# Layer 2 of a four-layer model: dense experts against experts over gathered tokens

## The chip, the cores and the metric

The kernel runs on one core of a Trainium2 chip. The metric is the device time of one execution in microseconds, the median of several runs. Five engines work side by side, each on its own stream of instructions in order: PE multiplies matrices into PSUM, DVE and ACT do elementwise work and read PSUM, POOL does elementwise work in SBUF and issues indirect transfers, SP issues the other transfers. Semaphores tie them together.

## What is computed

The input x has 16 batches of 256 tokens and 256 features; everything is float32. Four layers follow each other, each an attention part and a feed-forward part added to x: layer 0 with top-2 routing over eight experts of limited capacity, layer 1 with eight gated experts and a shared one, layer 3 with a projection in simulated 8-bit floats. The feed-forward part of layer 2 is itself a causal self-attention followed by four unlike experts, of which each token uses two:

```python
logits = jnp.nan_to_num(xf @ gate_w.T)
probs = jax.nn.softmax(logits, axis=-1)
topv, topi = jax.lax.top_k(probs, K)                    # K = 2 of E = 4
topv = topv / (topv.sum(-1, keepdims=True) + 1e-08)
wts = jnp.zeros((N, E), x.dtype).at[jnp.arange(N)[:, None], topi].add(topv)
o0 = _gelu(xf @ e0_up.T) @ e0_down.T
o1 = jax.nn.silu(xf @ e1_w1.T) * (xf @ e1_w2.T) @ e1_down.T
o2 = _gelu(_gelu(_gelu(xf @ e2_l1.T) @ e2_l2.T) @ e2_l3.T) @ e2_l4.T
o3 = _gelu(_gelu(xf @ e3_down.T) @ e3_up.T) @ e3_out.T
moe = wts[:, 0:1] * o0 + wts[:, 1:2] * o1 + wts[:, 2:3] * o2 + wts[:, 3:4] * o3
moe = moe.reshape(B, T, C).at[:, :, :M].set(0.0)        # M = 64
return x + moe
```

## The kernel before

Each layer is a software pipeline over batches. A hand-written list, `order`, has entries (position, function, lag, arguments). The loop runs over steps s and calls each function in order of position for batch s minus lag, where that batch exists. In the layers with such a list PE, DVE, ACT and POOL execute exactly in this order of calls; transfers on SP keep their program order too. A lag of 2 means that the function works on a batch two steps after that batch's lag-0 functions.

In layer 2 (L1097 on) a step holds, for the newest batch, the cross attention (`X[b]`, a `Heads32` object: `exps`, `added`, `values`, then `x_back`, which transposes its result back and adds it to x), then at lag 0 `statistics`, `norm`, `turned`, `project`, `head_squares`, `head_scale`, `heads_k`, `heads_q` and four `maxima` of the causal self-attention. At lag 1 follow four `exps`, `values`, `back`, `out_project` (which leaves the normalised tokens in `hh`) and `experts_in` (their transpose `xf`). The gate's logits, `route` and `routed` (the weights `wts`) come at lags 1 to 2.

`exps` masks the causal triangle after the exponential, by an affine select on POOL; `maxima` masks before, by a bf16 matmul of a triangle with the identity. `added` sums the exponentials of the two halves of the keys on POOL, so that `values` needs the product with ones once; without it, `values` multiplies both halves.

The experts are `work`, a list of units. Every unit fills one PSUM bank with two `f_part` calls and empties it with `f_end`: gelu on ACT, or silu as a tanh on ACT and two products on DVE, or for the last layer of an expert `f_add`, which multiplies by `wts` and adds into x. All four experts run on all 256 tokens of a batch, at lag 2, spread evenly over the step's positions. Their weights are streamed in 14 parts per batch by `fetch` and `part` through seven buffers `fw`. Four PSUM banks serve attention, two the experts. `f_done` stores x to DRAM (`xd2`) at lag 3.

Layer 3 loads x with `prepare`, four steps ahead of its attention. Layer 1's results reach layer 2 as in-flight row gathers, `x_fetch`, from `yslots`, an indirect transfer on POOL. Layer 0's `load` also clears DRAM buffers for later scatters, from a tile `zero`.

Of the kernel before, what the change touches and what calls it, by code (L numbers as in the profile page):

```python
# [36 lines left out]
def tile_kernel(ctx: ExitStack, tc: tile.TileContext, a, out):  # L37
# [72 lines left out]
    yslots = keep.tile([NBLK * BLK, D], F32, name="yslots")  # L110
    idx1 = ct([P, 2, NT], "idx1", U32)
# [287 lines left out]
    with ExitStack() as l01:  # L399
# [30 lines left out]
        with ExitStack() as l0:  # L430
# [47 lines left out]
            def load(b):  # L478
# [10 lines left out]
                if 2 <= b < 6:  # L489
                    for k in range(2):  # L490
                        dma(xe[k][(b - 2) * 1024 : (b - 1) * 1024, :].rearrange("(p r) d -> p (r d)", p=P), zero)
                        if b == 2:
                            dma(ye[k][8 * CAP :, :], zero[0:1, :D])
                if 6 <= b < 6 + (NBLK * BLK + 1023) // 1024:
                    rows = xslots[(b - 6) * 1024 : min((b - 5) * 1024, NBLK * BLK), :]
                    dma(rows.rearrange("(p r) d -> p (r d)", p=P), zero[:, : rows.shape[0] * 2])
# [120 lines left out]
            def scatter(b, n):  # L617
# [17 lines left out]
                (0, exps, 0, 0), (1, q_stats, -2), (2, back, 1, 0), (3, maxima, -1, 1), (4, scatter, 3, 1),  # L635
                (5, back, 1, 1), (6, values, 0, 0), (7, t_stats, 1), (8, exps, 0, 1), (9, queries, -1, 0, QMs),
                (10, maxima, -1, 2), (11, slots, 2), (12, values, 0, 1), (13, t_norm, 1), (14, exps, 0, 2),
                (15, q_norm, -2), (16, scatter, 5, 4), (17, maxima, -1, 3), (18, turned, 1), (19, values, 0, 2),
                (20, queries, -2, 0, QTs), (21, exps, 0, 3), (22, router, 1), (23, maxima, -2, 0), (24, route, 1),
                (25, load, -3), (26, queries, -1, 1, QMs), (27, values, 0, 3), (28, queries, -2, 1, QTs),  # L640
                (29, scatter, 3, 2), (30, v_heads, -2),
# [476 lines left out]
    with ExitStack() as l2:  # L1118
# [6 lines left out]
        wts = t2([P, NT, 4], "wts")  # L1125


        with ExitStack() as l2a:
            ca = l2a.enter_context(tc.tile_pool(name="ca", bufs=1))
            wp = at[0] = l2a.enter_context(tc.tile_pool(name="at2", bufs=2))  # L1130
            ring[0] = rings(at[0], 16)
# [11 lines left out]
            n2w = col(a["n2_w"], 2, "n2w", ca)  # L1143
# [17 lines left out]
            trif = ta([P, P], "trif")  # L1161
            V.memset(trif, 0.0)
            G.affine_select(trif, trif, [[-1, P]], ALU.is_ge, -MASKED, base=0, channel_multiplier=1)
            tri2 = ta([P, 2, P], "tri2", BF16)
            for i in range(2):
                V.tensor_copy(tri2[:, i, :], trif)
# [28 lines left out]
            def x_load(b):  # L1195
                ys[b] = []
                xs[b] = wp.tile([P, 2, D], F32, name="x2", tag="x2", bufs=6)
# [109 lines left out]
            def mask(sc, j, t):  # L1307
                T.matmul(
                    sc[:, :, t * P : (t + 1) * P], lhsT=ident_bf, rhs=tri2,
                    start=True, stop=False, skip_group_check=True,  # L1310
                )

# [9 lines left out]
            def exps(b, u):  # L1322
                pT = pTs[b, u] = probs(u // 2, u % 2, QMs[b], KTs[b], 32, 0.0, 1.0, None, None, True)
                q0 = u % 2 * P

                for e in pT:
                    G.affine_select(  # L1327
                        e[:, :, q0 : q0 + P], e[:, :, q0 : q0 + P], [[0, 2], [1, P]], ALU.is_ge, 0.0, base=0, channel_multiplier=-1
                    )
# [21 lines left out]
            def out_project(b):  # L1351
                xn, ss = xcs.pop(b), small(2, "ss")
                hh = hhs[b, 1] = wp.tile([P, 2, D], F32, name="hh", tag="hh")
# [23 lines left out]
            def experts_in(b):  # L1377
                xfs[b] = wp.tile([P, 2, S], F32, name="xf", tag="xf")
                transposed(xfs[b], hhs.pop((b, 1)), n2w, A)

            def gates(b):
                p, xf = ptr(), xfs[b]
# [19 lines left out]

            def routed(b):

                pr, w, m = routes.pop(b), wts[:, 2 * b : 2 * b + 2, :], small(2, "rm")
# [3 lines left out]
                oh = [sm.tile([P, 2, 4], F32, name=f"oh2{k}", tag=f"oh2{k}", bufs=2) for k in range(2)]  # L1409
                m12 = [small(2, f"m12{k}", bufs=2) for k in range(2)]  # L1410
                top2(pr, 2, 4, oh, m12)
                V.scalar_tensor_tensor(m, m12[0], 1e-8, m12[1], ALU.add, ALU.add)
                V.reciprocal(m, m)
                for k in range(2):
                    V.tensor_tensor(m12[k], m12[k], m, ALU.mult)
                    V.tensor_tensor(oh[k], oh[k], m12[k].unsqueeze(2).to_broadcast([P, 2, 4]), ALU.mult)
                V.tensor_tensor(w, oh[0], oh[1], ALU.add)
                V.tensor_scalar(w[:, :, 1], w[:, :, 1], 0.5, None, ALU.mult)
# [4 lines left out]
                ("e0_upT", 2, 0, 512), ("e2_l1T", 2, 0, 512), ("e0_downT", 4, M, D), ("e1_w1T", 2, 0, 512),  # L1423
                ("e2_l2T", 4, 0, 256), ("e2_l2T", 4, 256, 512), ("e1_w2T", 2, 0, 512), ("e1_downT", 4, M, D),
                ("e2_l3T", 4, 0, 256), ("e2_l3T", 4, 256, 512), ("e3_downT", 2, 0, D),
                ("e2_l4T", 4, M, D), ("e3_upT", 2, 0, 512), ("e3_outT", 4, M, D),
# [3 lines left out]
            def fetch():  # L1430
                n, k, n0, n1 = parts[len(fw) % len(parts)]
                t = fp.tile([P, 1024], F32, name="fw", tag="fw", bufs=7)
# [4 lines left out]
            def part(b, i):  # L1437
                n = len(parts) * b + i
                while len(fw) < min(n + 6, len(parts) * B):
# [3 lines left out]
            hs = {}  # L1443
# [4 lines left out]
            def f_up(b, p, j, src, i, f):  # L1448

                w = part(b, i)  # L1450
                src = xfs[b] if src is None else hs[src]
                src = [src[:, c, :] for c in range(2)] if not isinstance(src, list) else [h[:, c, :] for h in src for c in range(2)]
# [346 lines left out]
```

## Time and profile before

| | |
|---|---|
| median of 3 runs | 3467.52 us (3456.1 to 3470.55) |
| the profiled execution | 3460.77 us |
| its span, first to last instruction | 3459.1 us |
| PE busy | 3117.0 us, 90% |
| PE weight loads busy | 2283.7 us, 66% |
| DVE, ACT, POOL busy | 1578.2, 1162.5, 1064.4 us |
| moved by DMA | 332.87 MB, 96 GB/s on average |

By busy time and the layers' first instructions, layer 0's attention runs to about 430 us, its experts to 900, layer 1 to 1556, layer 2 to 2969, layer 3 to the end. Busy time is summed per engine over the span or over a window. A group's row gives line, engine, operation, output and input tiles, shape and count, then busy time, mean nanoseconds of one, and the idle time before it with what ended it. Matmul instructions overlap, so a group's busy time is less than its count times its mean; a float32 product is two instructions in these rows. Times are from one execution.

### The profile page before, as it was taken

What the parts mean: (1) busy time and instruction counts of PE and PEld (TensorE: products, weight loads), DVE (VectorE), ACT (ScalarE), POOL (GpSimd) and SP (SyncE); (2) the same over time, 40 slices, a digit from 0 to 9 for tenths busy, and PEclk for the clock granted to TensorE, in tenths of its full rate; (3) what the DMA queues carried; (4) which work ended last, traced back from release to release, by engine and by line L of the source; (5) the groups of instructions that cost most, each with busy time, mean ns of one, the idle gap of its engine ahead of it and who ended that gap; (6) DMA issues with size and microseconds to landing.
All of it is one profiled execution on the core that took longest, in us unless ns stands there. A gap on an engine that the chain in (4) does not pass through costs nothing. (4 is left out here: it accounts for less than half of the span.)

```text
span 3459.1 us, 54867 instructions
## 1 busy us (share of the span) xinstructions
PE 3117.0 (90%) x21640; PEld 2283.7 (66%) x21640; DVE 1578.2 (46%) x3920; ACT 1162.5 (34%) x2085; POOL 1064.4 (31%) x1643
## 2 busy tenths in 40 slices
PE   7999599999677999995799999999999999699983
PEld 4666366666465578882477777777777778566751
DVE  6777511000475322223445455555455442277766
ACT  3555321111122111111245555554555544122221
POOL 2455600000473510002233333333333221155552
PEclk9999799999988999996799999999999999899995
DMA  6411222121232366653023333333333234310101
GB/s 229 152 51 43 71 73 72 64 74 40 76 115 78 123 217 200 192 172 107 13 78 105 100 106 108 110 100 105 97 103 98 88 91 127 128 31 27 30 7 49
DMA packets 262132, 332.87 MB, mean 96 GB/s; under 512 B 20891, under 2 KB 214091, under 8 KB 259700
## 3 DMA queue, kind: packets, MB, share of 16 engines
q1 hardware_dynamic: 249588, 296.59, 27.2%
q0 software_dynamic: 12288, 32.78, 2.8%
q8 instruction: 171, 2.80, 0.3%
q14 instruction: 85, 0.70, 0.1%
HBM read 259.29 MB, written 70.80 MB: 95 GB/s over the span
## 5 line engine op out<-in xcount | busy, mean ns | idle before, releaser
L1454 PE MATMUL pf<-hf,fw 128*128 128x256 f32 x1280 | 302.5, 380 | 0.0
L1454 PE MATMUL pf<-xf,fw 128*128 128x256 f32 x1152 | 290.8, 390 | 0.0
L252 ACT ACTIVATE big<-pmm 128x512 f32<-128x512 f32 (+1 forms) x512 | 237.1, 549 | 116.3 <-PE pmm L245 115.7
L1454 PEld LDWEIGHTS pf<-hf,fw 128*128 128x128 f32 x1280 | 234.6, 190 | 31.8 <-issue 4.8
L1454 PEld LDWEIGHTS pf<-xf,fw 128*128 128x128 f32 x1152 | 207.7, 190 | 55.0 <-issue 27.7
L780 PE MATMUL pmm<-xiT,w 128*128 128x512 f32 x512 | 225.4, 598 | 5.4 <-DVE xiT L134 5.3
L1327 POOL TENSOR_SCALAR_AFFINE_SELECT big<-big 128x256 f32<-128x256 f32 x256 | 104.8, 426 | 393.4 <-ACT big L252 386.6
L788 PE MATMUL pacc<-w,h 128*128 128x256 f32 x1024 | 223.6, 379 | 0.0
L788 PEld LDWEIGHTS pacc<-w,h 128*128 128x128 f32 x1024 | 194.6, 190 | 33.3 <-issue 7.7
L816 POOL DMA_INDIRECT y<-ye,idx x64 | 65.5, 1024 | 479.3 <-issue 479.3
L789 DVE COPY yo<-pacc 128x256 f32<-128x256 f32 x64 | 27.2, 425 | 402.2 <-PE pacc L788 402.2
L305 DVE TENSOR_REDUCE max<-pmm 128x2 f32<-128x512 f32 x256 | 158.9, 683 | 91.6 <-PE pmm L223 91.1
L1481 PE MATMUL pf<-fw,hf 128*128 128x192 f32 x1024 | 191.2, 331 | 0.2
L1318 DVE TENSOR_REDUCE qpad<-pmm 128x2 f32<-128x256 f32 (+1 forms) x256 | 124.9, 551 | 137.6 <-PE pmm L223 137.6
L522 DVE TENSOR_REDUCE qpad<-pmm 128x2 f32<-128x512 f32 x256 | 158.9, 684 | 54.6 <-PE pmm L223 54.4
L338 POOL TENSOR_TENSOR big<-big 128x512 f32<-128x512 f32 x128 | 158.6, 1273 | 73.3 <-ACT big L252 73.3
L780 PEld LDWEIGHTS pmm<-xiT,w 128*128 128x128 f32 x512 | 96.2, 191 | 124.4 <-issue 112.3
L1481 PEld LDWEIGHTS pf<-fw,hf 128*128 128x128 f32 x1024 | 165.6, 190 | 13.7 <-issue 11.9
L1212 POOL DMA_INDIRECT y<-yslots,idx x64 | 66.7, 1043 | 315.2 <-DMA yslots<-yb 301.7
L355 DVE RECIPROCAL rT<-pacc 128x256 f32<-128x256 f32 x64 | 112.1, 1751 | 94.8 <-PE pacc L347 94.8
L1466 ACT ACTIVATE hf<-pf 128x512 f32<-128x512 f32 x176 | 104.8, 595 | 124.2 <-PE pf L1454 123.6
L146 POOL TENSOR_SCALAR rsq<-mv 128x2 f32<-128x2 f32 x128 | 25.1, 196 | 337.2 <-DVE mv L164 318.8
(383 smaller groups left out, 6164.7 us busy)
## 6 DMA issues: line engine op xcount, KB each, us to landing
w<-in_w_dram SPq DMA_DIRECT2D x16, 1024.0 KB
fw<-in_e_upT_dram SPq DMA_DIRECT2D x32, 512.0 KB
fw<-in_e_l2T_dram SPq DMA_DIRECT2D x32, 512.0 KB
fw<-in_e_l3T_dram SPq DMA_DIRECT2D x32, 512.0 KB
wg<-in_w_gate_dram SPq DMA_DIRECT2D x39, 352.0 KB
wu<-in_w_up_dram SPq DMA_DIRECT2D x39, 352.0 KB
fw<-in_e_downT_dram SPq DMA_DIRECT2D x32, 384.0 KB
wd<-in_w_down_dram SPq DMA_DIRECT2D x39, 256.0 KB
```

The costliest lines, as they stand in the source:

```text
L252: A.activation(e[:, :, q0:], sc[j], AF.Exp, bias=bias, scale=scale)
L305: V.tensor_reduce(self.m[:, t, j, :], sc, AX.X, ALU.max, negate=True)
L338: G.tensor_tensor(r, self.pT[0][j], self.pT[1][j], ALU.add)
L355: V.reciprocal(rT, p[:, 1, :])
L522: V.tensor_reduce(qps[b][t][:, 8 * cp + j : 8 * cp + j + 5 : 4, 17], sc, AX.X, ALU.max, negate=True)
L780: T.matmul(p, lhsT=w1[:, c, f * P : (f + 1) * P], rhs=xiT[:, c, :], start=(c == 0), stop=(c == 1))
L788: T.matmul(p[:, :D], lhsT=hT[f][:, s * P : (s + 1) * P], rhs=w2[:, f, :], start=(f == 0), stop=(f == 7))
L1318: V.tensor_reduce(qp[:, 8 * cp + j : 8 * cp + j + 5 : 4, 16], sc, AX.X, ALU.max, negate=True)
L1327: G.affine_select(e[:, :, q0 : q0 + P], e[:, :, q0 : q0 + P], [[0, 2], [1, P]], ALU.is_ge, 0.0, base=0, channel_multiplier=-1)
L1454: T.matmul(p[:, j * S : (j + 1) * S], lhsT=w[:, c, f * P : (f + 1) * P], rhs=x, start=(c == 0), stop=(c == len(src) - 1),)
L1466: A.activation(f_hidden(to, f), p, AF.Gelu)
L1481: T.matmul(p[:, t * S : t * S + D - M], lhsT=hs[src][f // 2][:, f % 2, t * P : (t + 1) * P], rhs=w[:, f, :], start=(f == 0), stop=(f == 3),)
```

## The change

The experts of layer 2 get only the tokens that chose them. DRAM buffers `xe2` and `ye2` hold 4096 rows for each expert; each pair of batches has 256 of them. `places` counts, by two matmuls with `before` and `ones`, each token's slot in the regions of its two experts. `scatter` writes the tokens to these slots by four indirect transfers a batch; `f_in` reads the 256 rows of a pair and an expert, `f_turned` transposes them, and the units run over them. `f_out` stores the results to `ye2`. A region that runs over continues in the next pair's 256 rows. Rows beyond 2048 are left to a new stage after the loop, which loads all expert weights and works in pieces of 128 to 512 rows, each behind a test of the expert's count.

Expert 2 runs at even steps and the other three at odd ones, at lags 4 and 5, some ends one step on. The loop has three more steps. In layer 3, `fetch` gathers each token's two result rows and `chosen` adds them, weighted. Further, `exps` masks by matmul, `added` is not called in layer 2, and the lists of layers 0 and 3 have new positions and lags.

```diff
+    xe2 = keep.tile([4 * REG, D], F32, name="xe2")
+    ye2 = keep.tile([4 * REG, D - 64], F32, name="ye2")
...
+                dma(xe2[b * 1024 : (b + 1) * 1024, :].rearrange("(p r) d -> p (r d)", p=P), zero)
+                n0 = b // 4 * REG + REG // 2 + b % 4 * 512
+                dma(ye2[n0 : n0 + 512, :].rearrange("(p r) d -> p (r d)", p=P), zero[:, : 4 * (D - 64)])
...
-                (0, exps, 0, 0), (1, q_stats, -2), (2, back, 1, 0), (3, maxima, -1, 1), (4, scatter, 3, 1),
...
+                (0, scatter, 3, 1), (1, back, 1, 0), (2, maxima, -1, 1), (3, back, 1, 1), (4, exps, 0, 1),
...
-            ring[0] = rings(at[0], 16)
+            ring[0] = rings(at[0], 12)
...
+            def maskT(sc):
+                T.matmul(sc[:, :, :P], lhsT=ident_bf, rhs=tri2[:, 1], start=True, stop=False, skip_group_check=True)
...
-                pT = pTs[b, u] = probs(u // 2, u % 2, QMs[b], KTs[b], 32, 0.0, 1.0, None, None, True)
-                q0 = u % 2 * P
-
-                for e in pT:
-                    G.affine_select(
-                        e[:, :, q0 : q0 + P], e[:, :, q0 : q0 + P], [[0, 2], [1, P]], ALU.is_ge, 0.0, base=0, channel_multiplier=-1
-                    )
+                pTs[b, u] = probs(u // 2, u % 2, QMs[b], KTs[b], 32, 0.0, 1.0, None, maskT, True)
...
+            def places(b):
...
+                T.matmul(p[:, 0:16], lhsT=before, rhs=ohf, start=True, stop=True)
+                T.matmul(p[:, 16:32], lhsT=ones, rhs=ohf, start=True, stop=True)
...
+                V.tensor_scalar(cum[:, 0, :], taken[0], float(b // 2 * S), None, ALU.max)
+                for i in range(4):
+                    V.tensor_tensor(cum[:, i + 1, :], cum[:, i, :], p[:, 16 + 4 * i : 20 + 4 * i], ALU.add)
+                taken[0] = cum[:, 4, :]
...
+            def scatter(b, t):
+                for k in range(2):
+                    G.memset(apart, 0.0)
+                    i = G.indirect_dma_start(
+                        out=xe2, out_offset=bass.IndirectOffsetOnAxis(ap=idx2[:, k, 2 * b + t : 2 * b + t + 1], axis=0),
+                        in_=hhs[b, 1][:, t, :], in_offset=None,
+                    )
...
+            def f_in(b, e):
+                x = xis[e] = fp.tile([P, 2, D], F32, name="xi2", tag="xi2", bufs=2)
+                dma(x, xe2[f_rows(b, e), :].rearrange("(p r) d -> p r d", r=2))
+
+            def f_turned(b, e):
+                x = fp.tile([P, 2, S], F32, name="xf2", tag="xf2", bufs=2)
+                transposed(x, xis.pop(e), n2w, A)
+                hs["x", e] = [x]
...
-            def f_add(b, p, e):
-                for t in range(2):
-                    xt = xs[b][:, t, M:]
-                    V.scalar_tensor_tensor(xt, p[:, t * S : t * S + D - M], wts[:, 2 * b + t, e : e + 1], xt, ALU.mult, ALU.add)
+            def f_out(b, p, e):
+
+                y = fp.tile([P, 2, D - M], F32, name="yo2", tag="yo2", bufs=2)
+                A.activation(y, p.rearrange("p (t d) -> p t d", t=2)[:, :, : D - M], AF.Copy, scale=0.5 if e == 1 else 1.0)
+                dma(ye2[f_rows(b, e), :].rearrange("(p r) d -> p r d", r=2), y)
...
+            def f_part(b, odd, u, j):
+                if b % 2 == odd:
+                    if j == 0:
+                        banks[odd, u] = f_bank()
+                    work[odd][u][1](b, banks[odd, u], j)
...
+                (0, f_end, 5, 1, 8), (1, f_part, 5, 1, 9, 0), (2, gates, 2), (3, x_step, 0, "exps", 1),
+                (4, f_of, 4, 0, f_in, 2), (5, f_of, 4, 1, f_in, 0), (6, f_of, 4, 1, f_in, 1), (7, f_part, 5, 1, 9, 1),
+                (8, route, 2), (9, f_end, 5, 1, 9), (10, f_part, 5, 1, 10, 0), (11, f_part, 5, 0, 5, 1),
+                (12, x_norm, -1), (13, x_fetch, -2, 0, 0), (14, x_out, 2), (15, x_step, 0, "values", 0),
...
+                (49, f_part, 4, 1, 1, 0), (50, places, 2), (51, f_end, 4, 0, 0), (52, f_part, 4, 0, 1, 0),
...
-            for s in range(-2, B + 3):
+            for s in range(-3, B + 5):
...
+        with ExitStack() as l2e:
+            fx = l2e.enter_context(tc.tile_pool(name="fx2", bufs=2))
+            psums(l2e, "ps2e", 4, 2, 2)
...
+                FW[n] = weight(fx, n, k * P, n0, n1, bufs=1)
+            cnt = fx.tile([1, 4], I32, name="cnt2", tag="cnt2", bufs=1)
+            V.tensor_copy(cnt, taken[0][:1, :])
...
+            def more(e, many, n0, sizes):
+                if sizes:
+                    with tc.If(many > n0):
+                        tokens(e, n0, sizes[0])
+                        more(e, many, n0 + sizes[0], sizes[1:])
+
+            for e in range(4):
+                many = nc.values_load(cnt[0:1, e : e + 1], min_val=0, max_val=REG)
+                more(e, many, REG // 2, [128, 128, 256, 512, 512, 512])
...
+        def fetch(b, t, k):
+            y = ys[b, t, k] = wp.tile([P, D - M], F32, name="y3", tag="y3", bufs=8)
+            G.indirect_dma_start(
+                out=y, out_offset=None, in_=ye2,
+                in_offset=bass.IndirectOffsetOnAxis(ap=idx2[:, k, 2 * b + t : 2 * b + t + 1], axis=0),
+            )
+
+        def chosen(b):
+            for t in range(2):
+                for k in range(2):
+                    i, x = 2 * b + t, xs[b][:, t, M:]
+                    V.scalar_tensor_tensor(x, ys.pop((b, t, k)), wk2[:, k, i : i + 1], x, ALU.mult, ALU.add)
```

## The prediction

> **What bounds the kernel now.** I read the busy rows over the span first, then the busy time in stretches cut where layer 2 begins and ends, then the groups of instructions by line, then the timeline at the layer's edges.
>
> ```profile
> PE   7999599999677999995799999999999999699983
> ACT  3555321111122111111245555554555544122221
> PEclk9999799999988999996799999999999999899995
> ```
>
> Slices of 86.5 us. PE is the engine at nine tenths almost everywhere. Layer 2 is slices 19 to 34; at its front (slices 18, 19) PE and its granted clock both sag.
>
> ```profile
> core 0: us, PE busy (x) PEld busy (x) DVE busy (x) ACT busy (x) POOL busy (x), PEclk, DMA share, GB/s
> 1615.00:1685.00 70.00, 47.60 (x287) 24.82 (x286) 30.30 (x69) 13.28 (x25) 12.73 (x21) 0.63 0.07 18
> 1685.00:1759.00 74.00, 60.75 (x469) 38.61 (x470) 37.84 (x101) 29.62 (x59) 28.66 (x49) 0.82 0.08 24
> 1759.00:2808.00 1049.00, 1038.43 (x8400) 812.39 (x8400) 533.60 (x1433) 534.45 (x924) 345.08 (x592) 1.00 0.33 101
> 2808.00:2969.00 161.00, 160.17 (x1043) 135.33 (x1041) 44.84 (x139) 66.19 (x114) 27.47 (x57) 1.00 0.33 102
> 2969.00:3000.00 31.00, 1.12 (x5) 0.88 (x6) 6.10 (x22) 0.00 (x0) 3.66 (x5) 0.58 0.81 272
> ```
>
> The cuts are the transposes of x_back, which runs once per step (timeline and L1239's own row, first and last start):
>
> ```profile
> 1614.80 0.48 PE L1239 MATMUL ptr<-ident,uT 128*128 128x128 f32 x1
> 1684.90 0.33 PE L1239 MATMUL ptr<-ident,uT 128*128 128x128 f32 x1
> 1759.32 0.60 PE L1239 MATMUL ptr<-ident,uT 128*128 128x128 f32 x4
> L1239 PE MATMUL ptr<-ident,uT x64: 272/273/476, 1614.8 to 2808.5; 128*128 128x128 f32 x64
> ```
>
> Steps 2 to 15, with experts, take (2808.5-1759.3)/13 = **80.7 us**, PE busy 79.9 of them: PE-bound. The two steps before, attention without experts, take 70.1 and 74.4 us although they hold about 30 us of PE work (79.9 less 49.4 for the experts). There PE waits for one batch's chain (exps, values, x_back, statistics, norm, projections, head scale, transposes, maxima) at a clock of 0.63 and 0.82. The experts fill these holes for nothing today. That decides what halving them is worth.
>
> ```profile
> L1454 PE MATMUL pf<-hf,fw 128*128 128x256 f32 x1280 | 302.5, 380 | 0.0
> L1454 PE MATMUL pf<-xf,fw 128*128 128x256 f32 x1152 | 290.8, 390 | 0.0
> L1481 PE MATMUL pf<-fw,hf 128*128 128x192 f32 x1024 | 191.2, 331 | 0.2
> L1327 POOL TENSOR_SCALAR_AFFINE_SELECT big<-big 128x256 f32<-128x256 f32 x256 | 104.8, 426 | 393.4 <-ACT big L252 386.6
> L338 POOL TENSOR_TENSOR big<-big 128x512 f32<-128x512 f32 x128 | 158.6, 1273 | 73.3 <-ACT big L252 73.3
> L347 PE MATMUL pacc<-big,ones 128*32 128x256 f32 x208 | 22.7, 384 | 0.0
> L1308 PE MATMUL pmm<-tri,ident_bf 128*128 128x256 bf16 x208 | 31.6, 272 | 0.0
> ```
>
> (The last two rows from 1759 to 2808.) The three expert groups sum to 784.5 us of PE, 642 of them in those 13 steps, 49.4 each.
>
> **PE per full step of layer 2.** Removed: half the experts, 24.7 us, since 512 tokens now cost one pass over 256 slots. Added: transposes of gathered rows, 32 instructions a pair at 0.150 (L190, 15.6 us for 104), 2.4 a step; the causal mask of exps as 16 bf16 matmuls at 0.152 (L1308), 2.4, in place of 16 affine selects on POOL; the new order has no "added" steps in layer 2, so values multiplies both halves of the exponentials by ones, 16 more at 0.109 (L347), 1.75; places, 4 short ones at 0.12 (L1385), 0.5. Sum: 79.9-24.7+2.4+2.4+1.75+0.5 = **62.2 us**.
>
> **The other engines per step.** ACT: 41.1-3.9 (half of gelu and tanh)+1.9 (f_turned, four 0.47 us evacuations)+0.9 (f_out)+1.3 (9 table loads by the new order's sequence of exp and gelu; now 104 in 13 steps, 8, at 1.28) = 41.3. DVE: 41.0-3.3 (f_add)-1.4 (half the gating)+1.0 (places, less the old weighting) = 37.4. POOL: 26.5-6.8 (selects)-5.1 (adds)+4.6 (four scatters at 1.04 and memsets) = 19.2. None comes near 62. The shorter attention chain loses 0.4 us behind each exps and 5 us of POOL adds.
>
> **Step length.** I estimate the warm chain from the 70.1 us step: 47.6 busy PE us at clock 0.63 are about 30 warm, so 18 fewer, less 5: near 48. But in-order engines put expert groups of 1 to 4 us between its roughly 14 PE hops, some 14 us. So chain and PE load meet at 62. Bounds: 63 (today's 98.9% busy) and 74.4 (as long as the attention-only step). I take **65**, nearer to PE, whose row in the full steps shows hardly a wait. [...] by the row, gaps stay short while experts run, and I apply the cold clock only to the filling steps.
>
> **Fill and drain.** Experts now come four steps later: attention alone runs in steps 0 to 3, not 0 and 1. From the first x_back to the last: 66+3x67 (70 and 74 less the shorter chain) + 11x65 = 982, against 1193.7. After the last x_back, now 160: rest of step 15, 50; step 16 (attention's tail with pair 6's first half) 45; step 17, 30; the last pair alone, 54 of PE (49.4+4.8) with 8 of stalls behind its layers: 187. Net **-185 us** (1169 against 1354). Bounds of this term: -240 at 63 and warmer filling, -70 at 74.4.
>
> **Queues.** f_in waits on SP for the scatters of the step before; behind it are weight fetches (five parts ahead, some 45 us at 14 parts per two steps), x_load and x_out. The scatters wait on POOL for places; behind them stand the row fetches and head_scale's memset, with 43 us of POOL idle a step to absorb it. Weight traffic halves, so DMA (0.33) falls. Cost: nothing; a late scatter would show as PE waiting at f_turned.
>
> **The tail l2e**, which no row shows. 6400 KB of weights come first on SP; at the 350 to 388 GB/s measured while layer 2's first transfers land (1571 to 1584) that is 18 us, and the first rows queue behind them. From the reference's own routing, the slots run to 2366, 1967, 2078, 2172 (gaps in short pairs included): beyond 2048 there are bodies of 128, 128, 256 (expert 0), 128 (2), 128 (3). Warm, the first holds 4 transposes at 0.15, 16 products at 0.12 and 8 down at 0.19, 4 us, and 2 for its evacuations; so 6+6+11+15+7 = 45 for the five. Lower end 18+45 = 63. [...] Nearest row: the joint before layer 3, 31 us with PE idle for loads. [...] I take **+100**, the middle: some bodies will overlap[...].
>
> **The rest.** Layer 3: 64 row fetches (1.04 on POOL) and 64 multiply-adds (0.41 on DVE); POOL goes from 12 to 16, DVE from 16.5 to 18 of a 22 us step whose PE is 98% busy. One fetch stands between the adds that values waits for: 0.5 a step, 8, and 5 at its start: **+13** (0 to 25). Layer 0: 22.5 MB of zeros at DMA share 0.31 over 430 us; uncovered they would cost some 60 us, covered only the crowded start, **+5**. Its reordered steps I cost at 0 (-15 to +15): PE there is 96% busy after 100 us.
>
> **Sum.** -185+100+13+5 = **-67**. The profiled run took 3460.8 (span 3459.1): 3394. The median of the runs is 6.8 higher: **3400 us**.
>
> **Rivals.**
> 1. PE stays the only bound: steps of 63 (-22), filling 5 shorter three times (-15), drain -10, tail 60 (-40), layer 3 -8: **3305**. For: ACT and DVE have a third to spare. Against: 70 us steps at 30 us of PE.
> 2. Slower: the attention chain sets every step. Its price is the measured 74.4: 11 x 9.4 = +103, **3503**. It decides from 65+67/11 = 71 us a step. Against: those steps ran at 0.63 to 0.82 of the clock, and with experts it is 1.00.
> 3. The tail eats the gain: 156 for 100 gives **3456**; from 167 on nothing is left.
> 4. The pass isn't halved, because slots run over: 512 tail slots for expert 0 are 1/8 of a 4096-token pass, already in the tail.
>
> **How the numbers follow.** Forecast 0.52 (own range 3340 to 3460), rival 1 0.22, rival 2 0.13, rival 3 0.13. 3300 to 3485 leaves out rival 1's far half-tail and most of rival 2, some 0.2. About 0.5% (17 us) is what a measurement can tell from no change. Faster 0.49+0.22+0.05 = 0.76 (most of rival 3 lies within); same 0.09; slower 0.11 from rival 2 and 0.04 from a longer tail.
>
> **What would show it.** Spacing of x_back 65 with PE near 95% in full steps, and three steps of 67 before them; 640 and 576 instructions for L1454's two forms inside the loop; PE waits naming DVE or ACT rather than none; a stretch after the loop with PE mostly idle, near 100 us. I am wrong if steps are above 71 or the tail is above 167, or if PE waits for gathered rows.

## The result, and the profile after

The changed kernel takes **3439.8 us** in the median (eight runs, 3425.7 to 3452.8), the kernel before 3468.8 in runs on the same chip: a ratio of 0.9918, 95% interval 0.9891 to 0.9945. The gain is 29 us where 67 were forecast; the sign and the range were right, the size was not. Run again on another chip, the changed kernel had a ratio of 0.9944 (0.9927 to 0.996). The profiled execution is the longest of its runs, with a span of 3451.1 us, 8 less than the kernel before. The experiments ran on several chips, on which the kernel before took 3457 to 3545 us; so they are compared by their ratios to it, or by steps within one trace.

First the busy tenths of PE and its granted clock over 40 slices of 86 us:

```profile
PE   7999599999677999995777898998989897599983
...
PEclk9999799999887999996778999999999998799995
```

Layer 2's steps with experts, slices 23 to 31 or so, no longer show a row of nines on PE; the filling steps ahead of them (slices 18 to 22) hold four steps where there were two, with a low clock as before. The busy time of each engine in four stretches puts numbers to that: the filling steps 0 to 3, the ten steps with all their experts, the rest of the loop, and the tail (columns as before: stretch, length, busy time and instructions of each engine, clock, DMA share, GB/s):

```profile
core 0: us, PE busy (x) PEld busy (x) DVE busy (x) ACT busy (x) POOL busy (x), PEclk, DMA share, GB/s
1613.00:1893.00 280.00, 207.97 (x1704) 122.25 (x1700) 137.59 (x375) 83.30 (x174) 65.18 (x112) 0.79 0.09 29
1970.00:2704.50 734.50, 671.20 (x5827) 473.87 (x5824) 376.97 (x1072) 395.92 (x706) 194.38 (x332) 0.99 0.27 85
2704.50:2879.40 174.90, 162.75 (x1075) 133.85 (x1073) 39.52 (x141) 74.97 (x144) 29.10 (x51) 1.00 0.48 159
2879.40:2952.60 73.20, 41.52 (x212) 37.05 (x212) 3.88 (x10) 16.02 (x40) 0.02 (x1) 0.73 0.08 23
```

Ten full steps take 734 us, **73.4 each** (73.3 to 74.0 in the four traces whose full steps are the same: this one, e7, e8 and e11); the forecast had 65. PE is busy 67.1 us of each (62.2 computed), DVE 37.7 (37.4), ACT 39.6 (41.3), POOL 19.4 (19.2). So no engine is the bound by its busy time, and the load of three engines was forecast to within 2 us. The tail is 73 us (forecast 100), the stretch from the last x_back to the loop's end 175 (187). x_back's first transposes in the timeline, here of three of the ten steps, show two lengths in turn:

```profile
1970.04 0.33 PE L1254 MATMUL ptr<-ident,uT 128*128 128x128 f32 x1
2041.58 0.33 PE L1254 MATMUL ptr<-ident,uT 128*128 128x128 f32 x1
2116.31 0.33 PE L1254 MATMUL ptr<-ident,uT 128*128 128x128 f32 x1
2187.85 0.33 PE L1254 MATMUL ptr<-ident,uT 128*128 128x128 f32 x1
```

The five steps of the one kind take 71.5 us each, the five of the other 73.3 to 78.0; even and odd steps hold different expert layers. The groups of the ten full steps (name and count, busy time, mean ns, idle before), and who PE waited for in them (total us, times, longest):

```profile
L1519 PE MATMUL pf<-hf,fw 128*128 128x256 f32 x400 | 103.7, 397 | 7.4 <-ACT hf L1531 7.4
L1519 PE MATMUL pf<-xf,fw 128*128 128x256 f32 x360 | 94.0, 390 | 0.0
L258 ACT ACT_TABLE_LOAD x41 | 52.6, 1283 | 52.7 <-PE pmm L251 52.2
L1531 ACT ACT_TABLE_LOAD x40 | 51.3, 1283 | 0.6
L353 PE MATMUL pacc<-big,val 128*32 128x256 f32 x320 | 41.0, 412 | 3.1 <-DVE rm L1420 2.3 <-ACT big L258 0.8
L353 PEld LDWEIGHTS pacc<-big,val 128*32 128x32 f32 x320 | 12.4, 113 | 26.7 <-ACT big L258 17.1 <-issue 5.1 <-PE ptr L276 3.4
```

```profile
PE pf L1546 <- ACT hf L1531: 10.1, 5, 2.0
PE ptr L276 <- ACT QT L147: 8.7, 10, 0.9
PE pmm L1323 <- DVE qpad L1336: 8.7, 30, 0.3
PE pf L1519 <- ACT hf L1531: 7.4, 10, 1.3
```

The pass over the experts is halved as said (640 and 576 instructions of the two forms in all). PE's waits are many and short, none over 2.0 us, on both ACT and DVE. One row explains two fifths of the 4.9 us by which PE is busier than computed: the 32 products by val a step take 0.128 us each, where they took 0.067 in the full steps before:

```profile
L347 PE MATMUL pacc<-big,val 128*32 128x256 f32 x416 | 27.8, 385 | 0.0
```

This is a wait that the count of busy time hides. In the timeline the second sixteen of a step mostly take 1.07 us, as before, and the first sixteen 2.7 to 3.0; ahead of them the weight loads wait 17.1 us in the ten steps for ACT's exponentials (the PEld row above).

The tail's timeline on PE (start, duration, count, and in brackets the idle time before it and its end):

```profile
2879.95 0.41 PE L1661 MATMUL ptr<-ident,xi 128*128 128x128 f32 x2 [0.64 <-DMA xi<-xe]
...
2883.52 1.47 PE L1693 MATMUL pacc<-e_downT,h 128*128 128x192 f32 x8
2887.88 0.44 PE L1661 MATMUL ptr<-ident,xi 128*128 128x128 f32 x2 [2.90 <-DMA xi<-xe]
...
2891.15 2.53 PE L1693 MATMUL pacc<-e_downT,h 128*128 128x192 f32 x8
2897.16 1.11 PE L1661 MATMUL ptr<-ident,xi 128*128 128x128 f32 x4 [3.48 <-DMA xi<-xe]
...
2904.52 2.76 PE L1693 MATMUL pacc<-e_downT,h 128*128 128x192 f32 x16
2917.63 0.66 PE L1661 MATMUL ptr<-ident,xi 128*128 128x128 f32 x2 [10.35 <-DMA xi<-xe]
...
2930.18 1.47 PE L1693 MATMUL pacc<-e_l4T,h 128*128 128x192 f32 x8
2938.81 0.66 PE L1661 MATMUL ptr<-ident,xi 128*128 128x128 f32 x2 [7.17 <-issue]
...
2946.22 2.31 PE L1693 MATMUL pacc<-e_outT,h 128*128 128x192 f32 x8
```

Five bodies, as the routing said. From the first transpose of each to the end of its last product they take 44.7 us; the other 28.5 lie between and behind them. The first starts within a microsecond of the loop's end: SP had issued the weights during the loop's last steps, where the DMA share is 0.48. Each later body loads its rows only inside its conditional. SP's timeline shows when (the last store of one body, L1698, and the load of the next body's rows, L1656):

```profile
2885.41 0.32 SPq L1698 DMA_DIRECT2D ye<-yo  x1
2885.88 0.33 SPq L1656 DMA_DIRECT2D xi<-xe  x1
...
2907.91 0.32 SPq L1698 DMA_DIRECT2D ye<-yo  x1
...
2914.25 0.32 SPq L1656 DMA_DIRECT2D xi<-xe  x1
```

Within one expert the load follows the store by 0.5 us and PE starts 2.0 (and, for the third body, 2.6) us after it. From one expert to the next, 6.3 us (and 2.9 before the last body) pass ahead of the load, and 3.4 (3.9) behind it. So the rows are only a part of the two longest gaps, 10.35 and 7.17 us; the rest holds the tests that fail, and no row splits it further.

The whole account, after less before, in the two profiled executions: start of layer 2 -1.3; first x_back to last -102.7 (1091.0 against 1193.7); from there to the loop's end +14; tail +73; layer 3 with its joint +9 (498.5 against 489.7). Sum -8.

### The profile page after: what moved, and what is told of

It is laid out like the page before. It is cut to its first block, busy times and chain, and to the rows that moved or that the text cites. A ratio compares the mean times of both kernels' runs of the same rounds, so it can differ in the third digit from the quotient of the medians.

```text
span 3451.1 us, 53628 instructions
## 1 busy us (share of the span) xinstructions
PE 2961.7 (86%) x20828; PEld 2085.4 (60%) x20828; DVE 1553.2 (45%) x3950; ACT 1125.6 (33%) x2094; POOL 1024.4 (30%) x1517
## 5 line engine op out<-in xcount | busy, mean ns | idle before, releaser
L152 POOL TENSOR_SCALAR rsq<-mv 128x2 f32<-128x2 f32 x128 | 25.6, 200 | 506.0 <-DVE mv L170 460.6
L1519 PE MATMUL pf<-hf,fw 128*128 128x256 f32 x640 | 161.1, 393 | 11.0 <-ACT hf L1531 10.2
L1519 PE MATMUL pf<-xf,fw 128*128 128x256 f32 x576 | 146.6, 389 | 4.0 <-ACT xf L147 4.0
L1519 PEld LDWEIGHTS pf<-hf,fw 128*128 128x128 f32 x640 | 117.4, 193 | 41.6 <-ACT hf L1531 16.1
L276 PE MATMUL ptr<-ident,qpad 128*128 128x128 f32 x512 | 86.4, 294 | 51.3 <-DVE qpad L179 21.2
L791 ACT ACTIVATE h<-pmm 128x512 f32<-128x512 f32 x128 | 76.4, 597 | 154.6 <-PE pmm L789 154.6
L267 PE MATMUL pacc<-big,vpad 128*32 128x256 f32 (+1 forms) x2048 | 126.7, 364 | 0.0
L353 PE MATMUL pacc<-big,val 128*32 128x256 f32 x1024 | 106.4, 423 | 18.0 <-DVE rm L1420 7.8
L1519 PEld LDWEIGHTS pf<-xf,fw 128*128 128x128 f32 x576 | 102.9, 190 | 28.6 <-issue 8.9
L1458 POOL DMA_INDIRECT xe<-h,idx x64 | 65.4, 1021 | 178.9 <-DVE idx L1451 145.7
```

Of the source, the lines that this page charges most:

```text
L267: T.matmul(O[32 * j : 32 * j + 32, i, q0:], lhsT=lhsT(kc, 8 * cp + 4 * i + j), rhs=pT[j][:, i, q0:], start=(kc == 0 and i == 0), stop=(kc ...
L276: T.transpose(p[:, c, :], src[:, h0 + 4 * c : h0 + 4 * c + 4, :].rearrange("p h d -> p (h d)"), ident)
L353: T.matmul(p[32 * j : 32 * j + 32, k, :], lhsT=ones32 if k else self.val[:, kc, 32 * h : 32 * h + 32], rhs=self.sum[j][:, i, :] if k and s ...
L791: A.activation(h, p, AF.Gelu_apprx_tanh)
L1519: T.matmul(p[:, j * S : (j + 1) * S], lhsT=w[:, c, f * P : (f + 1) * P], rhs=x, start=(c == 0), stop=(c == len(src) - 1),)
```

## The experiments

The question was why a full step takes 73 us with no engine full. Theories: (a) PE's load sets it; (b) one step's data must pass through the step before; (c) a chain of short waits through engines that work in a fixed order, tied together by table loads, drains and PSUM banks.

**Less for PE.** Each contraction in the loop's expert layers keeps only its last part:

```diff
-                for c, x in enumerate(src):
-                    T.matmul(..., start=(c == 0), stop=(c == len(src) - 1))
+                c, x = len(src) - 1, src[-1]
+                T.matmul(..., start=True, stop=True)
...
-                for f in range(4):
-                    T.matmul(..., rhs=w[:, f, :], start=(f == 0), stop=(f == 3))
+                T.matmul(..., rhs=w[:, 3, :], start=True, stop=True)
```

> Every expert product in layer 2's loop keeps only its last part of the contraction (it sums over 128 of 256 or 512 features), so waits, ACT, DVE, POOL and DMA work stay and PE loses 28 x 0.259 + 18 x 0.261 + 24 x 0.195 = 16.6 us of the 67.1 us that it is busy in a full step of the changed kernel. If PE's load sets the step (73.4 us between two x_back): about 57 us a step, some 220 to 250 us off the total with the last steps. If the attention chain sets it: 70 us or more a step, and 20 to 50 us off the total, from the last steps, where there is no attention.

Ratio 0.9787 (0.9768 to 0.9807). The ten full steps in the trace:

```profile
1951.60:2651.71 700.11, 564.36 (x5125) 355.68 (x5121) 378.60 (x1071) 393.91 (x705) 194.05 (x332) 0.96 0.28 89
```

PE is busy 10.7 us less a step (16.6 were computed; the clock is 0.96 instead of 0.99) and idle 13.6, yet the step loses only 3.4 (70.0). (a) falls as a bound by itself: with five sixths of PE's busy time the step still takes 70 us.

The two traces also show where the rest went. Follow the chain back from the x_back behind the ten full steps to the one ahead of them, at each instruction to what released it or to the one before it on its engine; this reading of the releasers is inferred, not tested. In the changed kernel a step's 73.3 us of chain are PE 52.1 (15.9 of it expert products), ACT 12.8, DVE 6.3, no busy engine 2.0. In e1 they are PE 39.5, ACT 13.9, DVE 14.4 and 2.1. So a round through DVE, nearly as long, takes over when PE's part shrinks.

**No table loads.** The loop's GELU becomes a tanh:

```diff
-                A.activation(f_hidden(to, f), p, AF.Gelu)
+                A.activation(f_hidden(to, f), p, AF.Tanh)
```

> The gelu of layer 2's experts in the loop is replaced by tanh, which shows no table load of its own beside exp in either trace, so the 9 table loads of a step (1.28 us each, 11.5 us of ACT) should go and nothing else. If the loads lie on the chain that sets the step, 3 to 8 us a step and 40 to 100 us in all; if PE's load sets the step, under 1.5 us a step and under 25 us in all.

Ratio 0.9806 (0.9787 to 0.9826).

```profile
1944.58:2643.26 698.68, 645.02 (x5824) 467.43 (x5821) 375.10 (x1071) 290.22 (x625) 194.04 (x332) 1.00 0.29 89
```

All 81 loads are gone, 10.6 us of ACT a step; the step is 3.6 shorter (69.9). PE's busy time falls by 2.6 us a step, though its instructions are the same; most of that is the wait inside the products by val, which cost 0.071 us each again:

```profile
L353 PE MATMUL pacc<-big,val 128*32 128x256 f32 x320 | 22.7, 385 | 2.5 <-DVE rm L1420 2.5
```

**POOL takes work back from PE.** e3 adds layer 2's "added" steps to the list, so that POOL sums the exponentials as before; e4 puts POOL's affine selects back in place of exps' mask products:

```diff
+                (3.1, x_step, 0, "added", 0), (3.2, x_step, 0, "added", 1), (3.3, x_step, 0, "added", 2), (3.4, x_step, 0, "added", 3),
```

```diff
-                pTs[b, u] = probs(u // 2, u % 2, QMs[b], KTs[b], 32, 0.0, 1.0, None, maskT, True)
+                pT = pTs[b, u] = probs(u // 2, u % 2, QMs[b], KTs[b], 32, 0.0, 1.0, None, None, True)
+                q0 = u % 2 * P
+                for e in pT:
+                    G.affine_select(
+                        e[:, :, q0 : q0 + P], e[:, :, q0 : q0 + P], [[0, 2], [1, P]], ALU.is_ge, 0.0, base=0, channel_multiplier=-1
+                    )
```

> The POOL adds of layer 2's exponentials come back right after exps 1, and with them the single product with ones: PE loses 6.7 - 3.9 = 2.8 us a step, POOL gains 5.1, and 5 us of adds stand between exps and values. If PE's load sets the step: 2 to 3 us a step less, 30 to 45 us in all. If the attention chain sets it: up to 5 us a step more, 0 to 75 us slower.

> The causal mask of exps goes back to POOL's selects after the exponential: PE loses 2.6 us a step, POOL gains 6.8, and each of four values waits some 0.5 to 1.5 us longer. If PE's load sets the step: 2 to 2.6 us a step less, 25 to 40 us in all. If the chain sets it: same or up to 30 us slower.

e3: 1.003 (1.0017 to 1.0042), full steps 75.4; e4: 0.9922 (0.9905 to 0.9938), 72.7. The sums by POOL cost 2 us a step although they relieve PE; the selects make it 0.7 shorter, no more than traces of the same steps differ. The prediction had charged these two items of the change 1.75 and 2.4 us of PE; in the length of a step the first gains 2, and the second costs 0.7 at most.

**One step more of slack.** Everything from the statistics on runs one step later, so that x_back and what follows it no longer stand in one step:

```diff
-                (29, statistics, 0), (30, x_queries, -1), (31, exps, 1, 1), (32, f_of, 4, 0, f_turned, 2),
+                (29, statistics, 1), (30, x_queries, -1), (31, exps, 2, 1), (32, f_of, 5, 0, f_turned, 2),
...
-            for s in range(-3, B + 5):
+            for s in range(-3, B + 6):
```

> Same work, one more step of distance: everything in layer 2's loop from statistics on (self-attention, routing, experts, x_out) runs one step later than x_back, with a sixth buffer for x and one more step in the loop. If one batch's chain through x_back, statistics and maxima sets the step (it stood at 70.2 us with 16.6 us of PE taken away), the step is cut into two shorter chains and falls towards PE's own load: 62 to 68 us, for 12 steps some 60 to 130 off, less 30 to 40 for the further step: 30 to 90 us faster than the changed kernel. If the step is set by the fixed order on the engines and not by that dependency, it stays at 72 to 74 us and the kernel is 30 to 70 us slower.

> The kernel with the split step, and POOL's adds of the exponentials and causal selects back in place of the second product with ones and the mask matmuls: PE loses 2.8 + 2.6 us a step, POOL gains 11.9. If the split has made PE's load the bound: 3 to 5.4 us a step less than the split kernel, 35 to 75 us in all. If a chain still sets the step, as in the changed kernel, where the adds alone cost 33 us: 10 to 40 us slower than the split kernel.

e5: 1.0013 (1.0004 to 1.0023); e6, with e3's and e4's edits too: 1.0096 (1.0079 to 1.0112). e5's full steps are 71.5 and 73.3 to 78.0 in turn, as without it; one more step makes the run longer. (b) falls: it isn't this dependence. Then eleven entries were moved by hand to where the slack should serve them, with a second buffer for QTx; e10 has e8's filler (below), in five steps, on top:

```diff
-                (2, gates, 2), (3, x_step, 0, "exps", 1), ... (15, x_step, 0, "values", 0), ... (26, x_back, 0), ...
+                (2, gates, 3), (44.5, x_step, 0, "exps", 1), ... (56.5, x_step, 0, "values", 0), ... (74.5, x_back, 0), ...
```

> The split kernel with eleven entries moved so that the cross attention of the newest batch (exps, values, x_back, its loads and gathers) no longer stands ahead of the self-attention of the batch before in the order of each engine, but between its links; one buffer more for QTx. Same work. If the step is a round through the fixed orders, cross attention's hops (about 25 us) and then self-attention's (about 45), the two run side by side: steps of 62 to 68 us, 60 to 130 us off the split kernel, and faster than the changed kernel by 30 to 90. If fragmented PE work (67.1 busy) and its short waits set the step, 71 to 74 us as before and no gain on the split kernel.

> The woven kernel with three unused bf16 matmuls at every place of an expert's part in steps 0 to 4, as in e8_warm, where they made three of the four steps 3 to 10 us shorter. 15 to 35 us less than the woven kernel if the clock lengthens those steps here too; no gain if its shorter chains keep the clock up by themselves.

1.022 (1.0203 to 1.0237) and 1.0145 (1.0128 to 1.0162): steps mostly of 75 to 85 us. My order was worse than the one in the change, so this pair says nothing on whether a better one exists. Beside them ran the changed kernel again:

> The changed kernel itself, as the yardstick on this chip: a ratio of 0.989 to 0.995 to the kernel before, steps of 71.5 and 74.8 us in turn.

0.9944; steps of 71.5 and 73.3 to 78.0, as in the first trace.

**Without the tail.** The five bodies are left out:

```diff
             for e in range(4):
-                many = nc.values_load(cnt[0:1, e : e + 1], min_val=0, max_val=REG)
-                more(e, many, REG // 2, [128, 128, 256, 512, 512, 512])
+                pass
```

> The changed kernel without the tests and the pieces behind them: the 512 + 128 + 128 slots beyond 2048 of experts 0, 2 and 3 are left out; the weights are still loaded. If the tail is serial, as its 73 us in the trace say: 65 to 80 us off the total. If layer 3's loads and gathers, which wait behind it, would take their time anyway: 30 to 50 us.

0.9718 (0.9698 to 0.9738). The changed kernel did not run on that chip; against its ratios elsewhere this is 0.020 to 0.023 less, 71 to 80 us. The trace is sharper: from the last x_back to layer 3's first product by wout pass 325.4 us in both traces of the changed kernel (2704.5 to 3029.9 in the first) and 250.4 here, 75 less.

```profile
L1858 PE MATMUL pmm<-wout,uT x128: 379/379/483, 3019.8 to 3357.0; 128*128 128x256 f32 x128
L1254 PE MATMUL ptr<-ident,uT x64: 272/300/332, 1681.1 to 2769.4; 128*128 128x128 f32 x64
```

The tail is serial: its 73 us are its price, and nothing behind it would have taken that time anyway.

**PE kept warm while the loop fills.** Three unused bf16 products behind every (absent) expert part of steps 0 to 3:

```diff
                     do(f, s - lag, *more)
+                    if f is f_part and 0 <= s < 4:
+                        spare = f_bank()
+                        for _ in range(3):
+                            T.matmul(spare[:, :256].rearrange("p (i q) -> p i q", i=2), lhsT=ident_bf, rhs=tri2[:, 0], start=True, stop=True)
```

> In steps 0 to 3, attention without experts, three bf16 matmuls into an unused bank stand at each of the 38 places of the experts' parts (0.11 us each warm, 12 us a step), and nothing else changes. If the low clock (0.79 on average there) is what makes these steps 64 to 75 us long: 5 to 15 us less each, 20 to 50 in all. If their length is the chain on the other engines: no gain, or up to 20 us slower for PE's added work.

0.9881 (0.9865 to 0.9898), some 0.004 to 0.006 below the changed kernel's ratios on other chips. The four steps between the first five x_backs, first in the changed kernel, then here:

```profile
1613.52:1682.51 68.99, 47.92 (x310) 26.09 (x306) 30.84 (x69) 13.38 (x24) 9.03 (x18) 0.63 0.07 20
1682.51:1746.81 64.30, 47.58 (x467) 28.55 (x463) 33.14 (x96) 23.31 (x50) 15.94 (x26) 0.92 0.09 28
1746.81:1821.59 74.78, 57.99 (x470) 35.24 (x466) 37.17 (x107) 23.30 (x50) 20.09 (x34) 0.77 0.10 31
1821.59:1893.35 71.76, 54.31 (x470) 32.38 (x466) 36.79 (x107) 23.31 (x50) 20.11 (x34) 0.83 0.11 36
```

```profile
1683.73:1744.60 60.87, 49.33 (x422) 31.40 (x421) 30.93 (x70) 13.46 (x24) 9.00 (x18) 0.89 0.09 25
1744.60:1807.42 62.82, 54.94 (x580) 36.78 (x576) 33.31 (x95) 23.30 (x50) 15.85 (x26) 1.00 0.09 29
1807.42:1872.26 64.84, 55.06 (x584) 37.15 (x580) 37.02 (x107) 23.29 (x50) 20.10 (x34) 1.00 0.12 36
1872.26:1940.64 68.38, 57.01 (x564) 36.86 (x560) 38.85 (x108) 23.29 (x50) 20.11 (x34) 0.95 0.12 38
```

This is the reading that matters most. The third row of e8 is attention alone, complete (107 DVE instructions, as in a full step), at full clock: **64.8 us**. The filler's own instructions are in it, 4.7 us of them on its chain followed back as above, so without them it may be 60. The complete steps without filler (the third and fourth of the changed kernel, of e11 and of e7) took 68.4 to 74.8 at clocks of 0.88 to 0.77; a straight line through these six leads to about 64 at 1.00, an estimate. So the warm chain is some 60 to 65 us, where the prediction had 48. In a full step without its 15.9 us of expert products the chain is 57.4.

**PSUM banks and VectorE's drains.** The loop's eight banks are four for scores, one for transposes, one for the values' accumulators and two for the experts. e12 takes one of the experts' banks away; e13 gives it to the transposes ("ps2", 4, 2, 1 in the line above the edit), e14 to the scores (5, 1, 1); e15 leaves the banks and lets layer 2's own maxima read 32 keys only:

```diff
-            pf2 = l2a.enter_context(tc.tile_pool(name="ps2_ffn", bufs=2, space=PSUM))
+            pf2 = l2a.enter_context(tc.tile_pool(name="ps2_ffn", bufs=1, space=PSUM))
```

```diff
-                    V.tensor_reduce(qp[:, 8 * cp + j : 8 * cp + j + 5 : 4, 16], sc, AX.X, ALU.max, negate=True)
+                    V.tensor_reduce(qp[:, 8 * cp + j : 8 * cp + j + 5 : 4, 16], sc[:, :, :32], AX.X, ALU.max, negate=True)
```

> The feed-forward of the loop has one PSUM bank instead of two, and one of the eight banks stays empty. It is the control for the next two runs. If the feed-forward's two banks are what lets its matmuls run ahead of ScalarE's evacuations, each of a step's 18 or so evacuated groups is now waited for: full steps of 76 to 82 us where the changed kernel has 73, the run 40 to 130 us longer than the changed kernel's 3440. If only the hops of attention count, steps stay within 1 us of 73.

> As the control, and the bank that was empty goes to the transposes, which have two banks then. If the transposes' one bank sets the step (some 18 groups a step go through it, each transposed and evacuated before the next may start), steps are 4 us or more shorter than the control's, and the run 60 us or more faster than it. If it isn't the bank, within 1 us a step and 15 us in all of the control.

> As the control, and the empty bank goes to the scores' pool: five banks, of which each block takes four at once. If the score blocks' banks set the step (12 blocks that each fill four banks and wait for four drains), one group of a block can be filled while the block before is drained: 1 to 3 us a step shorter than the control, 15 to 45 us in all. If not, within 0.5 us a step.

> Layer 2's self-attention maxima are taken over the first 32 keys of each score tile only, not over all; every matmul, bank and order is as in the changed kernel, so this changes that part of what is computed. VectorE has some 16 reductions a step of 128 x 4 x 128 or 4 x 256 elements, which become a quarter or an eighth as long: some 7 us a step less on VectorE. If the draining of the banks on VectorE is part of the round that sets the step, full steps fall from 73 to 66 to 69 us and the run by 60 to 110 us. If VectorE's time is hidden, as its 38 us of 73 would suggest, steps stay within 1 us and the run within 20 us of the changed kernel's 3440.

e12: 1.0886 (1.0852 to 1.092); e13: 1.0665 (1.0624 to 1.0706); e14: 1.072 (1.0691 to 1.0749). e12's full steps, and PE's longest waits in them:

```profile
2044.65:3034.47 989.82, 770.16 (x5825) 545.96 (x5821) 376.84 (x1071) 395.82 (x705) 194.09 (x332) 0.84 0.20 63
```

```profile
PE pf L1519 <- ACT hf L1531: 100.0, 45, 5.4
PE pf L1546 <- ACT hf L1531: 32.9, 10, 4.1
```

One bank less makes the step 99.0 us, 25.6 longer, where 3 to 9 were expected: PE now waits for ACT's evacuation ahead of the next expert group, up to 5.4 us at a time, and the clock falls to 0.84. A bank returned to the transposes takes off 4.4 us a step (94.6), one to the scores 3.2 (95.8); the first as was expected of a bank that counts (4 or more), the second a little above it (1 to 3). e15, ratio 0.98 (0.9771 to 0.9828), fell between its two forecasts:

```profile
2008.69:2722.09 713.40, 660.37 (x5825) 469.95 (x5821) 323.29 (x1070) 394.72 (x705) 194.44 (x332) 0.99 0.28 87
```

5.4 us of DVE less a step gives 2.1 (71.3), and the first four filling steps, where attention is alone, together 25 us against e12's on the same chip (245.9 against 271.3, the experts' banks being idle there).

**A second bank for the transposes without taking one.** e16 moves the first values step next to the second, so that its accumulator isn't held between; e17 then lets transposes and accumulators share two banks:

```diff
-(42, values, 1, 0),
...
-(75, values, 1, 1),
+(74.9, values, 1, 0), (75, values, 1, 1),
```

```diff
-            psums(l2a, "ps2", 4, 1, 1)
+            ps["acc"] = None
+            psums(l2a, "ps2", 4, 2, 0)
...
     def pacc():
+        if ps["acc"] is None:
+            return ptr()
```

> The first of layer 2's four steps of weighted values (list position 42) is moved to just ahead of the second (75), so that its PSUM bank is not held between them. It is the control for the next run. If the order of the list is of little weight, steps stay within 1 us of 73 and the run within 20 us of the changed kernel's 3440; the moved products are 1.7 us of TensorE work that no longer fills a hole, so 0 to 25 us slower is likelier than faster.

> As the control, and the transposes and the accumulators of the values take their tiles from one pool of two banks, in place of one bank each; so two transposing groups may be in flight at once, wherever no accumulator is open. If the passing of that one bank is part of the round that sets the full step, steps are 1 to 4 us shorter than the control's and the run 15 to 60 us faster than it. If the round goes through the feed-forward's banks and the engines' fixed orders alone, within 0.5 us a step and 10 us of the control.

e16: 0.9942 (0.9921 to 0.9962), steps 73.4; e17: 0.9834 (0.9811 to 0.9856), 72.3. The five steps ahead of the full ones and the ten full ones, in e16 and then in e17:

```profile
1607.13:1960.07 352.94, 269.66 (x2262) 165.55 (x2259) 175.23 (x482) 119.68 (x239) 85.33 (x146) 0.84 0.12 37
1960.07:2693.94 733.87, 667.84 (x5824) 474.84 (x5821) 376.07 (x1071) 395.25 (x705) 193.80 (x332) 0.99 0.27 85
```

```profile
1602.86:1936.49 333.63, 261.31 (x2258) 161.89 (x2258) 175.83 (x482) 119.58 (x239) 84.93 (x146) 0.85 0.13 39
1936.49:2659.34 722.85, 668.26 (x5824) 475.36 (x5820) 376.25 (x1071) 394.69 (x705) 193.72 (x332) 0.98 0.27 86
```

So 39 us between them (3441.7, 3402.6): 11 in the ten full steps, 19 in the five before them, the rest ahead of and behind them. The bank counts, mostly where attention is alone; whether the transposes or the accumulators gain by sharing isn't separated here. Both together, e17 and the filler of e8:

> The shared banks of e17 and the unused bf16 products of e8 in steps 0 to 3 together. Alone, e17 took 37 us off the changed kernel and e8 some 13. If the filling steps are long because TensorE's clock falls in its gaps, and the banks shorten the same steps by another way, they add in part: a ratio of 0.979 to 0.984 to the kernel before. If the shared banks have already taken the gaps, the filler adds nothing or costs up to 5 us: 0.983 to 0.986. Full steps stay at 72 us by both.

**0.9801** (0.9782 to 0.982), 3390.4 us against 3459.0: faster than both kernels, with the whole of the computation. The filler's part on top of e17 is about 11 us by the ratios, and the four filling steps are 9.9 us shorter in the traces (249.4 against 259.3); the intervals of the two ratios just overlap.

## Why the prediction was half right

- **The failed step** is the size of the warm chain: "47.6 busy PE us at clock 0.63 are about 30 warm, so 18 fewer, less 5: near 48", and from it "So chain and PE load meet at 62". The warm chain is 60 to 65 us. Three things made the 48 too short. The 70.1 us step that it was read from held 69 DVE instructions, where a complete attention step here has 107, as the windows' counts showed; in e8 the first complete step is 4 us longer than the first step. The shorter chain was put at 5 us and gave 1: the first step of the changed kernel took 69.0 us at the clock of 0.63, at which it took 70.1 before. And warming was put at 18, as if the whole step went by PE's clock; in e8 the same first step took 60.9 us at 0.89, 8 less than 69.0, or 13 less without the 5.2 us of filler on its chain (the clock wasn't quite full, so this part is the least certain).
- **Chain and expert groups** were put together rightly. The prediction had 48 and 14 between the hops, 62; the chain followed back has 57.4 and 15.9, 73.3. So the size of the chain is what failed, and PE's load of 62 is not what the step meets. Work taken off an engine came back as a third of itself or a little more: 3.4 of 10.7 us on PE (e1), 3.6 of 10.6 on ACT (e2), 2.1 of 5.4 on DVE (e15). That is neither a bound engine (all of it) nor a hidden one (none); the chains followed back in e1 and in the changed kernel fit several rounds of nearly the same length. That PSUM banks are among the hops is shown (e12 to e14, e17); the share of each other hop wasn't tested, nor whether a better order of the list exists.
- **Step length 65** was the term that lost the gain: its eleven steps took 811 us for 715, +96. Rival 2, the attention chain at 74.4 in every step, was nearest to what happened, 1 us off in its price; it had 0.13. Its total of 3503 stood too high because the tail and the drain came cheaper.
- **Fill** was nearly right: 66+3x67 = 267 against 280 here and 271 in e11. It was read from steps at a low clock, so the 48 isn't in it; in part it was luck, since the complete steps took 72 and 75 us and only the second, incomplete one fell below 67. The prediction tied the cold clock to PE's gaps. Short waits and a high clock go together in the full steps (longest PE wait 2.0 us, clock 0.99), long waits and a low clock in e12 (5.4 and 0.84) and in the first filling step (5.2 and 0.63). But the third filling step stands at 0.77 with no wait over 2.3 us, and the second step of the kernel before at 0.82 with none over 1.2. What lowers the clock there stays open.
- **Tail**: +100 forecast, 73 in the trace and 75 by e7 (the middle of the prediction's 63 and 156 would have been 110; the 156 was my estimate, and no row had shown it). The 18 us of weights that "come first on SP" fell away: SP issued them during the loop's last steps. The bodies took 44.7 us, as the lower sum had them (45); the 28.5 around them are late loads of rows, tests, and the last store.
- **Drain** 175 for 187, **layer 3** +9 for +13, **layer 0** -1 for +5: high by 12, 4 and 6. Waits for gathered rows, the queues' cost of nothing, and the counts of rival 4 went as said; PE shows no long wait at f_turned.
- The terms add up: -67 forecast, +96 for full steps, +13 fill, -27 tail, -12 drain, -4 and -6 for layers 3 and 0, and -1 left over from rounding: the -8 of the two traces. The medians differ by 29, since after's profiled execution is its longest, 13 above its median, and before's lies 8 below its own.

## What to carry to other kernels

Before you treat a stage as cover for another, find a step of it alone that is complete: count its instructions on an engine that the change doesn't touch, and measure it with the clock held up by filler. When several in-order engines pass few PSUM banks round, expect neither nothing nor everything from shortening one of them; here each gave back a third or a little more. A second bank that lets a producer run one group ahead can be worth as much as the work itself: here it was worth 25.6 us a step (99.0 against 73.4), and all the experts' products of a step keep PE busy for 26.0 us.

## What the runs showed of the hardware that I had not expected

- The loads of ACT's tables are absent from the ten full steps when tanh stands beside exp (e2: none, where the changed kernel has 81). The rows show 1.283 us for each load, and taking 8.1 of them out of a step saved 3.6 us, 0.44 each: about two thirds of a load was hidden.
- Busy time on PE can hold a wait for another engine. The same column-tiled products (128 rows by 32, 256 wide) are busy 0.067 us each in the kernel before, 0.128 in the changed one, where their weight loads wait for ACT's exponentials, and 0.071 in e2, where ACT has no tables to load.
- Unused products in the filling steps raised the granted clock from 0.63 to 0.92 (four steps) to 0.89 to 1.00 and shortened the run (0.004 to 0.006 of the ratio), though 4.7 us of them lie on the chain of e8's third step. The clock stood at 0.77 in a step whose longest PE wait was 2.3 us.
